# Four attention and gating layers on one core: group sums of the norm on VectorE, layer 3's values as 2x2 blocks, gamma folded into weights

## The chip, the cores and the metric

The kernel runs on one core of one Trainium2 chip. The metric is the device time of that core in microseconds (us), the median of three runs. The engines are TensorE (PE, matrix products; PEld is its weight load), VectorE (DVE), ScalarE (ACT), GpSimd (POOL) and SyncE (SP), whose queue issues nearly all of the transfers.

## The reference

The input is 16 samples of 256 channels by 32x32 positions in f32 (1024 positions a sample). Each sample passes through four layers:

- Layer 0: group norm (8 groups of 32 channels), attention over the 1024 positions with 256 channels, projection, and the sum with the input.
- Layer 1: a gate. The mean and the maximum over the channels pass through two 3x3 convolutions and a sigmoid, and the result multiplies every position.
- Layer 2: group norm and attention as in layer 0, with other weights.
- Layer 3: attention with 32-channel queries and keys, 256-channel values, a scalar gamma on the output, and the sum with the input. The kernel clips the exponentials of the scores.

```python
def _L0_conv_ref(x, gamma, beta, w_qkv, b_qkv, w_proj, b_proj):
    xn = group_norm(x, gamma, beta)                  # 8 groups of 32 channels
    q, k, v = jnp.split(einsum(xn, w_qkv) + b_qkv, 3, axis=1)
    attn = softmax(q^T k / sqrt(C))
    return einsum(attn v, w_proj) + b_proj + x
def _L1_conv_ref(x, w1, b1, w2, b2):
    weight3 = relu(conv3x3(concat[mean_c(x), max_c(x)], w1, b1))
    return x * sigmoid(conv3x3(mean_c(x) + max_c(x) + weight3, w2, b2))
def _L3_conv_ref(x, Wq, bq, Wk, bk, Wv, bv, gamma):
    ...
```

Layer 2 is as layer 0, with x + out at its end.

## The kernel before

**Streams.** The kernel is one program of generators. `sample(b)` computes a whole sample; each `yield` in it ends a step. Two streams run, `stream(0)` with the even samples and `stream(1)` with the odd ones, and `in_turn` takes a step of each in alternation; the second starts 30 steps (`OFFSET`) after the first. The steps set the order in which instructions are written; a scheduler of the framework then orders each engine's queue from it, and each engine runs its queue in order. `wait(n)` yields n empty steps, so that the other stream gets n steps ahead. The numbers of empty steps are the constants `W_PLANES`, `W_GATE1`, ..., `W_AV3` at the top. A round, in which each stream finishes one sample, repeats eight times.

**Products by seven.** `seven` (line 581) forms a product of 2x2 blocks with seven block products in place of eight, by sums of the left blocks (`s1`, `s2`, `s4`, and `s3`, which is formed in place of a block) and of the right ones (`t1`, `t2`, `t3`, `-t4`). It uses four PSUM banks (b, a, c, f); the results leave them by copies on ScalarE and by additions (`plus`) on VectorE. All of its matmuls are recorded at line 567 in `product`. In layers 0 and 2, `attend` uses it for `t` (x times the folded query-key weights), for `v` (values) and, in `logits`, for the scores of a half of the positions; `weighted` is the like for the product of the exponentials `e` with the values. Tiles whose names start with s, t or v and a bank letter (`sb_l`, `tc_l`, `va_l`) are these banks; `b_l`, `af_l`, `c_l` are those of `weighted`.

**The norm.** `group_norm` has three steps. VectorE takes statistics of each channel (`bn_stats`, `bn_aggr` into `mv`). A matmul with `gmat` (1/32 in 32x32 blocks) gives group means on every channel (`gm`, line 125); VectorE forms each channel's variance plus its squared distance from the group's mean (`d`); a second matmul sums that (`gv`, line 134). GpSimd raises to the power -1/2, and VectorE and ScalarE scale the tile. Each sample has two norms, one for layer 0 (`head`, which for sample b+2 runs in the steps of layer 3 of sample b) and one for layer 2.

**The way from tokens to channels.** The attention leaves its result with tokens in the partitions, in 32-wide strips. `turn` transposes 32x32 blocks on VectorE into a tile in slot `t` of the stream, and `send` moves the strips across partitions with one transfer for each pair of strips, sixteen in one call, from SBUF to SBUF (line 515). After layer 1 one call sends both halves; after layer 2 each half is sent when it is ready. Layer 3's tile of queries and keys (`qk`, line 1034) lies in the same slot `t`, so it may be written only when those transfers have read the slot.

**Layer 3.** `clipped_attend` (line 1028) projects a half with `w3r`, which holds the query weights twice and the key weights twice, so that each of four 32-partition groups has what it needs; ScalarE and VectorE copy queries and keys out to both partition halves (lines 1050 and 1057). The values are formed by `values_of` (line 525), eight block products without `seven`, and ScalarE multiplies them by gamma while copying (line 1061). The scores are four products of 32 rows and 512 columns at a time, in four banks (line 1074); ScalarE takes exponentials (1083) and VectorE clips them (1086).

Of the kernel before, what the change touches and what calls it, by code (L numbers as in the profile page):

```python
# [44 lines left out]
W_PLANES, W_GATE1, W_GATE2, W_SEND1 = 5, 3, 1, 8  # L45
W_NORM1, W_NORM2, W_NORM3, W_SEND2 = 6, 3, 2, 6
W_EXP, W_AV, W_AV3 = 2, 0, 0
# [11 lines left out]
class Const:  # L59


    def __init__(self, nc, pool, vecs, scal):
        self.vec = pool.tile([P, CC, NVEC], FP, name="vec")
        self.sc = pool.tile([P, NSCAL], FP, name="sc")
        self.dram = vecs, scal
        self.ident = pool.tile([P, P], FP, name="ident")
        make_identity(nc, self.ident)
        self.ones = pool.tile([P, P], FP, name="ones")
        nc.gpsimd.memset(self.ones, 1.0)

        self.gmat = pool.tile([P, P], FP, name="gmat")
        nc.gpsimd.memset(self.gmat, 0.0)
        for g in range(P // GROUP):
            s = slice(g * GROUP, (g + 1) * GROUP)
            nc.gpsimd.memset(self.gmat[s, s], 1.0 / GROUP)
        self.neg_half = pool.tile([P, CC], FP, name="neg_half")
        nc.gpsimd.memset(self.neg_half, -0.5)

        self.toep = pool.tile([P, 2 + NG, STRIP], FP, name="toep")
        self.neg_b2 = pool.tile([P, 1], FP, name="neg_b2")
# [28 lines left out]
def group_norm(nc, k, small, psum, ptag, xt, out, gamma, beta, nm, keep=None):  # L111
# [3 lines left out]
    mv = small.tile([P, CC, 2], FP, tag="mv", name=f"mv_{nm}")  # L115
    for c in range(CC):
# [4 lines left out]
        nc.vector.bn_aggr(mv[:, c, :], st[:, c, :, :])  # L121
    yield

    gm_ps = psum.tile([P, HALF], FP, tag=ptag, name=f"gm_{nm}")
    nc.tensor.matmul(gm_ps[:, :CC], k.gmat, mv[:, :, 0], start=True, stop=True)
    gm = small.tile([P, CC], FP, tag="gm", name=f"gms_{nm}")
    nc.vector.tensor_copy(gm, gm_ps[:, :CC])
    d = small.tile([P, CC], FP, tag="d", name=f"d_{nm}")
    nc.vector.tensor_tensor(d, mv[:, :, 0], gm, ALU.subtract)
    nc.vector.tensor_tensor(d, d, d, ALU.mult)  # L130
    nc.vector.tensor_tensor(d, d, mv[:, :, 1], ALU.add)
    yield
    gv_ps = psum.tile([P, HALF], FP, tag=ptag, name=f"gv_{nm}")
    nc.tensor.matmul(gv_ps[:, :CC], k.gmat, d, start=True, stop=True)
    ve = small.tile([P, CC], FP, tag="ve", name=f"ve_{nm}")
    nc.vector.tensor_scalar(ve, gv_ps[:, :CC], EPS, None, ALU.add)
    rstd = small.tile([P, CC], FP, tag="rstd", name=f"rstd_{nm}")
    nc.gpsimd.tensor_tensor(rstd, ve, k.neg_half, ALU.pow)
    a = small.tile([P, CC], FP, tag="a", name=f"a_{nm}")
# [61 lines left out]
def fast_path(nc, tc, k, bad, x, w_l0, w_l2, w_l3, qk_bias, v_bias, tap_idx, out):  # L201
# [7 lines left out]
    with ExitStack() as ctx:  # L209
# [8 lines left out]
        small = ctx.enter_context(tc.tile_pool(name="small", bufs=4))  # L218
        ps_m = ctx.enter_context(
# [56 lines left out]
        for g in range(G4):  # L276
            i = g // 2
# [112 lines left out]

        w3r = wts.tile([P, CC, P], FP, name="w3r")
        gam = k.sc[:, S_GAMMA : S_GAMMA + 1]

        def fold3():
            for g in range(G4):
                i = g // 2
                tc.keep_in_program_order(
                    nc.gpsimd.tensor_copy(
                        w3r[:, :, g * DQK : (g + 1) * DQK], w3[:, :, i * DQK : (i + 1) * DQK]
                    )  # L400
                )
            ps = bank("bias3")
            for c in range(CC):
                nc.tensor.matmul(
                    ps[:, CC : CC + 1],
                    w3r[:, c, :],
# [16 lines left out]
            nc.vector.tensor_scalar(qb[:PH], qb[:PH], DQK**-0.5, None, ALU.mult)  # L423
            nc.vector.tensor_tensor(bcol3, ps[:, :CC], vcol[:, 2, :], ALU.add)
            nc.vector.scalar_tensor_tensor(bcol3, bcol3, gam, bcol2, ALU.mult, ALU.add)
            in_strips(bcol3, bstrip3, "l3")

# [80 lines left out]
        def send(z, dst, halves):  # L508


            dst = dst.rearrange("p (h g) c n -> p g h (c n)", h=NH)
            for g in range(NG):
                for b in range(NG):
                    queue = nc.sync
                    queue.dma_start(  # L515
                        dst[b * STRIP : (b + 1) * STRIP, g, halves],
                        z[g * STRIP : (g + 1) * STRIP, halves, b],
                    )

        def values_of(src, t2, w, vt, nm):  # L520

            ps = bank(f"vps_{nm}_{t2}")
            for i in range(2):
                for c in range(CC):
                    nc.tensor.matmul(
                        ps[:, i * C : (i + 1) * C],
                        src[:, 2 * t2 + i, c],
                        w[:, c],
                        start=(c == 0),
                        stop=(c == CC - 1),  # L530
                    )
            dst = vt[:, 4 * t2 : 4 * t2 + 4, :P].rearrange("p (t j) c -> p t j c", j=CC)
            return ps.rearrange("p (t j c) -> p t j c", t=2, j=CC), dst
# [53 lines left out]
        def seven(go, copy, block, banks, left, right):  # L587
# [27 lines left out]
            go(left("s3"), right("t3"), b, fresh=False)  # L615
            plus(1, 1, b)
            copy(1, 0, b)
# [8 lines left out]
        def logits(left, tt, e, h, nm):  # L626
# [20 lines left out]
            for g in range(TPH // 2):  # L647
# [23 lines left out]
                for step, _ in enumerate(seven(go, copy, block, banks, left, right)):  # L671
                    if step >= 2:
                        m = (step - 2) * TPH + 2 * g
                        nc.scalar.activation(e[:, m : m + 2, :], e[:, m : m + 2, :], AF.Exp)  # L674
                    yield

        def weighted(e, vt, tv, y, ri, h, nm, last=None):
# [58 lines left out]
            nc.vector.tensor_tensor(s2, s1, s2, ALU.subtract)  # L736
            go(a(0, 1), vb(1, 0), af[:, 0])
            yield
            nc.vector.tensor_tensor(s4, s4, s2, ALU.subtract)
            go(a(1, 1), t4, af[:, 1])  # L740
            plus(lo, c1, af[:, 0])
# [119 lines left out]
        def checks():  # L861
# [6 lines left out]
            yield from alike(w3[:, :, 2 * DQK :], "l3")  # L868
            yield

        def attend(xt, y, weights, lane, nm, then):
# [3 lines left out]
            xs = slot("xs", lane, [P, 3, TPH, P], nm)  # L875
            s1, s2, s4 = (xs[:, i] for i in range(3))
            blocks = [[xt[:, half(h), c] for c in range(CC)] for h in range(NH)]
            s3 = blocks[1][0]
            nc.vector.tensor_tensor(s1, s3, blocks[1][1], ALU.add)
            nc.vector.tensor_tensor(s2, s1, blocks[0][0], ALU.subtract)  # L880
            nc.vector.tensor_tensor(s4, blocks[0][1], s2, ALU.subtract)
            nc.vector.tensor_tensor(s3, blocks[0][0], s3, ALU.subtract)
            left = factors(blocks, {"s1": s1, "s2": s2, "s3": s3, "s4": s4})

            def right_of(w, sums):
                return factors(
                    [[w[:, kk, j * P : (j + 1) * P] for j in range(CC)] for kk in range(CC)],
                    {
                        "t1": sums[:, 0],
                        "t2": sums[:, 1],  # L890
                        "t3": w[:, 0, P:],
                        "-t4": sums[:, 2],
                    },
                )
# [23 lines left out]

            def v_block(i, j):
                return vt[:, i * NT + j : (i + 1) * NT : CC, :P]  # L920

            def v_go(xb, wb, ps, fresh=True, lone=True):
                product(
                    [
                        (ps[:, i * P : (i + 1) * P], [(xb[:, i], wb)])
                        for i in range(TPH)
                    ],
                    fresh,
                    lone,
                )  # L930

            def v_copy(i, j, ps):
# [546 lines left out]
```

## Time and profile before

| | before |
|---|---|
| time, median of 3 (range) | 2776.7 us (2775.44 to 2781.42) |
| span of the profiled run, granted TensorE clock | 2772.2 us, 0.996 |
| HBM read, written | 36.02 MB, 16.78 MB |

The groups of instructions that the change touches (a table by line, engine, operation and shape):

| group | count | busy us | mean ns |
|---|---|---|---|
| `gm_l`, `gv_l` matmuls of two columns (125, 134) | 64, 64 | 9.2, 10.0 | 214, 226 |
| `qk` matmuls of 512 columns (1041) | 128 | 61.4 | 602 |
| `vps_l` matmuls of 256 columns (525) | 512 | 120.7 | 379 |
| `s` matmuls, 32 rows, 512 columns (1074) | 512 | 75.5 | 639 |
| ScalarE copies of queries (1050) | 64 | 43.5 | 680 |
| VectorE copies of keys (1057) | 64 | 48.4 | 756 |
| ScalarE copies of values with gamma (1061) | 64 | 43.7 | 684 |
| VectorE `bn_stats` (118) | 128 | 82.7 | 675 |
| ScalarE exponentials in layers 0 and 2 (674) | 256 | 270.2 | 1056 |
| transfers of `send`, 64 KB and 32 KB (515) | 256, 512 | | landing 2000, 1800 |

Times in such tables are busy time as the union of a group's instructions; [...]consecutive matmuls overlap, and what one costs is read from the distance between the starts of two.

### The profile page before, as it was taken

Reading aid. Unit: us, or ns where it says so; the run is one execution under the profiler, and the core shown is the slowest. Engines: PE = TensorE matmul, PEld = TensorE weight load, DVE = VectorE, ACT = ScalarE, POOL = GpSimd, SP = SyncE. Lnnn points to the kernel's source line nnn. Section 1 sums busy time; section 2 is a strip of 40 time slices with the busy share of each in tenths; the row PEclk is TensorE's granted clock in tenths of the full one; section 3 lists DMA queues with packets and bytes.
Section 4 is the critical chain, followed back from the end, with each engine's and each line's share of the span. In section 5 each row is a group of like instructions: output and inputs, shape, how many; then the busy total and the mean of one; then the engine's idle time right before and its main releaser. Section 6 shows DMA issues by size and latency. Waiting matters only on the chain.

```text
span 2772.2 us, 46004 instructions
## 1 busy us (share of the span) xinstructions
PE 2701.7 (97%) x18102; PEld 2360.8 (85%) x18102; DVE 2096.8 (76%) x4045; ACT 1319.3 (48%) x2650; POOL 56.3 (2%) x118
## 2 busy tenths in 40 slices
PE   7999999999999999999999999999999999999997
PEld 6888888888988888888788887888888888888886
DVE  7887786877778777777777868778686887777765
ACT  3444355444554445544454445454444544445443
POOL 1000000000000000000000000000000000000000
PEclk9999999999999999999999999999999999999999
DMA  4011111011110120110201102111011011100101
GB/s 112 1 31 31 39 31 32 23 31 42 28 39 22 28 60 9 39 39 16 54 12 35 39 16 54 24 23 39 23 47 31 16 39 31 39 16 16 28 20 32
DMA packets 133790, 89.43 MB, mean 32 GB/s; under 512 B 17856, under 2 KB 132800, under 8 KB 133568
## 3 DMA queue, kind: packets, MB, share of 16 engines
q1 hardware_dynamic: 131696, 85.11, 12.5%
q8 instruction: 145, 2.38, 0.4%
q10 hardware_dynamic: 1872, 1.31, 0.2%
q14 instruction: 77, 0.63, 0.1%
HBM read 36.02 MB, written 16.78 MB: 19 GB/s over the span
## 4 chain that ended last, share of the span: by engine, by line
PE 69%; DVE 15%; ACT 6%; SPq 5%; DMA 2%; issue 2%; POOL 1%; ACTq 0%; DVEq 0%
PE b_l L567 12%; PE af_l L567 10%; PE c_l L567 10%; PE sb_l L567 9%; PE sc_l L567 6%; SPq L515 5%; PE sf_l L567 3%; PE sa_l L567 3%; PE vb_l L567 3%; PE tb_l L567 2%; PE vc_l L567 2%; ACT e_l L674 2%; PE tc_l L567 2%; DVE xr L722 2%; PE s L1074 2%
## 5 line engine op out<-in xcount | busy, mean ns | idle before, releaser
L674 ACT ACTIVATE e_l<-e_l 128x1024 f32<-128x1024 f32 x256 | 270.2, 1056 | 165.6 <-DVE e_l L599 164.5
L668 ACT COPY e_l<-sb_l 128x512 f32<-128x512 f32 x384 | 220.4, 582 | 170.3 <-PE sb_l L567 106.3
L567 PE MATMUL sb_l<-t_l,x 128*128 128x256 f32 x1024 | 266.1, 388 | 0.7 <-ACT e_l L668 0.7
L567 PE MATMUL b_l<-vt,e_l 128*128 128x128 f32 x2048 | 258.7, 277 | 0.9
L567 PEld LDWEIGHTS b_l<-vt,e_l 128*128 128x128 f32 x2048 | 244.8, 192 | 12.8 <-issue 7.7
L567 PEld LDWEIGHTS sb_l<-t_l,x 128*128 128x128 f32 x1024 | 179.8, 191 | 48.7 <-ACT e_l L668 13.6
L567 PE MATMUL c_l<-tv,cb_l 128*128 128x129 f32 x1536 | 187.2, 274 | 0.0
L599 DVE TENSOR_TENSOR e_l<-sc_l,e_l 128x512 f32<-128x512 f32 x128 | 88.1, 689 | 127.4 <-PE sc_l L567 125.3
L567 PEld LDWEIGHTS c_l<-tv,cb_l 128*128 128x128 f32 x1536 | 181.5, 191 | 1.6
L746 ACT COPY acc_l<-c_l 128x256 f32<-128x256 f32 x96 | 35.8, 373 | 271.5 <-DVE ri_l L745 178.4
L1083 ACT ACTIVATE e<-s 128x512 f32<-128x512 f32 x256 | 137.0, 605 | 54.5 <-PE s L1074 54.3
L567 PEld LDWEIGHTS af_l<-vt,e_l 128*128 128x128 f32 x1024 | 123.3, 192 | 38.0 <-ACT e_l L674 26.5
L567 PE MATMUL af_l<-vt,e_l 128*128 128x128 f32 x1024 | 131.6, 278 | 21.6 <-ACT e_l L674 21.6
L471 ACT ACTIVATE xr<-xr,bstrip 128x128 f32<-128x128 f32 (+1 forms) x376 | 139.3, 436 | 3.2 <-DVE xr L478 2.6
L567 PEld LDWEIGHTS af_l<-tv,e_l 128*128 128x128 f32 x1024 | 121.2, 192 | 19.4 <-issue 19.0
L599 DVE TENSOR_TENSOR e_l<-sf_l,e_l 128x512 f32<-128x512 f32 x128 | 88.5, 691 | 61.4 <-ACT e_l L668 61.2
L567 PE MATMUL sc_l<-tc_l,xs_l 128*128 128x256 f32 x512 | 133.0, 382 | 0.0
L567 PE MATMUL sb_l<-tc_l,xs_l 128*128 128x256 f32 x512 | 132.5, 381 | 0.5 <-ACT e_l L668 0.5
L567 PE MATMUL sa_l<-t_l,x 128*128 128x256 f32 x512 | 132.1, 381 | 0.0
L567 PE MATMUL sc_l<-t_l,xs_l 128*128 128x256 f32 x512 | 131.5, 379 | 0.0
L567 PE MATMUL c_l<-vt,e_l 128*128 128x129 f32 x1024 | 127.8, 277 | 3.7 <-ACT acc_l L746 3.6
L567 PE MATMUL sf_l<-tc_l,x 128*128 128x256 f32 x512 | 131.4, 379 | 0.0
(238 smaller groups left out, 5768.7 us busy)
## 6 DMA issues: line engine op xcount, KB each, us to landing
xr<-in_x_dram SPq DMA_DIRECT2D x64, 256.0 KB, 4.9
x<-t_z SPq DMA_DIRECT2D x256, 64.0 KB, 2.0
x<-t_l SPq DMA_DIRECT2D x512, 32.0 KB, 1.8
x<-in_x_dram SPq DMA_DIRECT2D x62, 256.0 KB, 4.1
out_dram<-xr SPq DMA_DIRECT2D x124, 128.0 KB, 2.3
raw_l<-in_w_l_dram SPq DMA_DIRECT2D x1, 1024.0 KB, 6.9
raw_l<-in_w_l_dram SPq DMA_DIRECT2D x2, 256.0 KB, 5.7
raw_l<-in_w_l_dram ACTq DMA_DIRECT2D x2, 256.0 KB, 5.6
```

Source lines behind the costliest of these rows:

```text
L471: nc.scalar.activation(y[:, s, ts], y[:, s, ts], AF.Identity, bias=bias[:, s : s + 1])
L515: queue.dma_start(dst[b * STRIP : (b + 1) * STRIP, g, halves], z[g * STRIP : (g + 1) * STRIP, halves, b],)
L567: mm = nc.tensor.matmul(out, left, right, start=fresh and m == 0 and (lone or i == 0), stop=(m == len(pairs) - 1), skip_group_check=True,)
L599: nc.vector.tensor_tensor(dst, src, dst, ALU.add)
L668: nc.scalar.copy(block(i, j), ps.rearrange("p (m n) -> p m n", m=2))
L674: nc.scalar.activation(e[:, m : m + 2, :], e[:, m : m + 2, :], AF.Exp)
L722: nc.vector.scalar_tensor_tensor(to, acc[:, i, :].rearrange("p (s j) -> p s j", j=STRIP), ri[:, t : t + 1], y[:, :, t, :], ALU.mult, ALU.add,)
L746: nc.scalar.copy(acc[:, hi, c2], c[:, :, :P])
L1074: nc.tensor.matmul(ss[g], kk[gs, mm * P : (mm + 1) * P], q[gs, hs], start=True, stop=True,)
L1083: nc.scalar.activation(e[:, mm, :], ss[g], AF.Exp)
```

## The change

- **Norm.** The matmuls with `gmat` go. The channels' means and variances are put side by side in a tile of 32 columns (`moments`); VectorE's transpose turns each 32x32 block, so that the 32 channels of a group lie along a row; `bn_stats` and `bn_aggr` over the row give the mean and the variance of both columns; the result is spread over 64 columns and turned back. The group's variance is the mean of the variances plus the variance of the means. The aim is to free TensorE from a small product that waits for VectorE twice.
- **Layer 3's values** go through `seven` (`values`, shared with `attend`), with the left sums formed by `combine`. Gamma is multiplied into the value weights once, in `fold3`.
- **Layer 3's projections and scores.** `w3qk` has, for each of two pairs of position tiles, 64 output columns (queries and keys, in either order). Four products of 256 columns and 64 outputs fill the two partition halves of a bank. Queries are scaled in the weights. Scores come as eight products of 256 columns per four banks.
- **`send`** goes through a tile in DRAM: four transfers out, one of 4 KB rows back. Layer 1's two halves are sent one by one.
- **`logits` and `weighted`.** The last exponential of a half is split in two, block (1,1) first, and `weighted` uses block (1,1) before (1,0); in `seven` the last copy is written ahead of an addition.
- **Empty steps.** All of the W constants are set anew. `W_AV`, 0 before, is 2.

```diff
-W_PLANES, W_GATE1, W_GATE2, W_SEND1 = 5, 3, 1, 8
-W_NORM1, W_NORM2, W_NORM3, W_SEND2 = 6, 3, 2, 6
-W_EXP, W_AV, W_AV3 = 2, 0, 0
+W_PLANES, W_GATE1, W_GATE2, W_SEND1, W_NORM1, W_NORM2, W_NORM3, W_SEND2, W_EXP, W_AV, W_AV3 = 9, 1, 2, 4, 2, 10, 4, 7, 2, 2, 0
...
-        nc.vector.bn_aggr(mv[:, c, :], st[:, c, :, :])
+        nc.vector.bn_aggr(mv[:, 2 * c : 2 * c + 2], st[:, c, :, :])
+    nc.vector.transpose(row, mv)
     yield
-    nc.tensor.matmul(gm_ps[:, :CC], k.gmat, mv[:, :, 0], start=True, stop=True)
-    nc.vector.tensor_copy(gm, gm_ps[:, :CC])
-    nc.vector.tensor_tensor(d, mv[:, :, 0], gm, ALU.subtract)
-    nc.vector.tensor_tensor(d, d, d, ALU.mult)
-    nc.vector.tensor_tensor(d, d, mv[:, :, 1], ALU.add)
-    yield
-    nc.tensor.matmul(gv_ps[:, :CC], k.gmat, d, start=True, stop=True)
-    nc.vector.tensor_scalar(ve, gv_ps[:, :CC], EPS, None, ALU.add)
+    nc.vector.bn_stats(rst, row)
+    nc.vector.bn_aggr(rmv, rst)
+    nc.vector.tensor_copy(wide, rmv.unsqueeze(2).to_broadcast([P, 2, GROUP]))
+    nc.vector.transpose(
+        both.rearrange("p i n -> p (i n)"), wide.rearrange("p i n -> p (i n)")
+    )
+    gm = both[:, 0, 0 : 2 * CC : 2]
+    nc.vector.scalar_tensor_tensor(
+        ve, both[:, 0, 1 : 2 * CC : 2], EPS, both[:, 1, 0 : 2 * CC : 2], ALU.add, ALU.add
+    )
     nc.gpsimd.tensor_tensor(rstd, ve, k.neg_half, ALU.pow)
+    yield
...
+            wv3 = w3[:, :, 2 * DQK :]
+            nc.vector.tensor_scalar(wv3, wv3, gam, None, ALU.mult)
+            vc = right_sums(nc.gpsimd, wv3, "vc_l3")
+            folded["l3"] = wv3, vc
...
+            mid = dram.tile([n, P, NG, C], FP, tag=f"mid{n}", name=f"mid_{nm}")
             for g in range(NG):
-                for b in range(NG):
-                    queue.dma_start(
-                        dst[b * STRIP : (b + 1) * STRIP, g, halves],
-                        z[g * STRIP : (g + 1) * STRIP, halves, b],
-                    )
+                nc.sync.dma_start(
+                    mid.rearrange("h (b i) g n -> g i (h b) n", b=NG)[g],
+                    z[g * STRIP : (g + 1) * STRIP, halves].rearrange("i h b n -> i (h b) n"),
+                )
+            nc.sync.dma_start(
+                dst.rearrange("p (h g) c n -> p h (g c n)", h=NH)[:, halves],
+                mid.rearrange("h p g n -> p h (g n)"),
+            )
...
-                        nc.scalar.activation(e[:, m : m + 2, :], e[:, m : m + 2, :], AF.Exp)
+                        if step == 3 and g:
+                            for j in reversed(range(2)):
+                                part = block(1, j)
+                                nc.scalar.activation(part, part, AF.Exp)
+                        else:
+                            nc.scalar.activation(e[:, m : m + 2, :], e[:, m : m + 2, :], AF.Exp)
...
+            go(a(1, 1), t4, af[:, 1])
+            yield
             go(a(0, 1), vb(1, 0), af[:, 0])
-            yield
+            plus(lo, c1, af[:, 0])
             nc.vector.tensor_tensor(s4, s4, s2, ALU.subtract)
-            go(a(1, 1), t4, af[:, 1])
-            plus(lo, c1, af[:, 0])
...
                 for c in range(CC):
-                    nc.tensor.matmul(
-                        ps.rearrange("p (g n) -> p g n", g=TPH),
-                        w3r[:, c, :],
-                        xt[:, half(h), c],
+                    for i in reversed(range(2)):
+                        g0 = h * TPH + i * qt
+                        nc.tensor.matmul(
+                            ps[i * PH : (i + 1) * PH, : qt * P].rearrange(
+                                "p (g n) -> p g n", g=qt
+                            ),
+                            w3qk[:, c, i],
+                            xt[:, g0 : g0 + qt, c],
...
-                for t2 in range(h * TPH // 2, (h + 1) * TPH // 2):
-                    ps, dst = values_of(xt, t2, w3[:, :, 2 * DQK :], vt, f"l3_{b}")
-                    nc.scalar.activation(dst, ps, AF.Copy, scale=gam)
+                if h:
+                    combine(left)
+                yield
+                if not h:
+                    next(steps)
                     yield
+            yield from steps
...
+                    for j in range(2):
+                        for g, (_, _, blk) in enumerate(groups):
                             nc.tensor.matmul(
-                            ss[g],
-                            kk[gs, mm * P : (mm + 1) * P],
-                            q[gs, hs],
+                                ss[g][:, j * 2 * P : (j + 1) * 2 * P].rearrange(
+                                    "p (t g j) -> p t g j", t=TPH, g=2
+                                ),
+                                qk[gs, mh, 1 - blk, j * P : (j + 1) * P],
+                                qk[gs, h, blk].rearrange("p (g t j) -> p t g j", g=2, t=TPH),
```

## The prediction

> **What bounds the kernel now.** I read the page first (busy shares), then the table of groups by form, then TensorE's timeline in a steady stretch, to learn what a matmul costs when nothing is in its way, then the waits of every engine, and last the chain of waits, for the length of a round. The page, its busy shares:
>
> ```profile
> PE 2701.7 (97%) x18102; PEld 2360.8 (85%) x18102; DVE 2096.8 (76%) x4045; ACT 1319.3 (48%) x2650; POOL 56.3 (2%) x118
> ```
>
> TensorE is busy 97%, VectorE 76%, ScalarE 48%. A busy TensorE may still run below its pace, so the timeline of TensorE has to say what full pace is (start, length, instruction; the distance from one row's start to the next is the true cost):
>
> ```profile
> 1441.21 1.03 PE L567 MATMUL sb_l<-t_l,x 128*128 128x256 f32 x4
> 1442.08 1.03 PE L567 MATMUL sa_l<-t_l,x 128*128 128x256 f32 x4
> 1442.94 1.95 PE L567 MATMUL b_l<-vt,e 128*128 128x128 f32 x16
> 1444.72 1.03 PE L567 MATMUL sc_l<-tc_l,xs_l 128*128 128x256 f32 x4
> ...
> 1381.31 1.14 PE L1074 MATMUL s<-t_qk 32*128 32x512 f32 x8
> 1382.38 1.16 PE L567 MATMUL vb_l<-wvp_l,x 128*128 128x128 f32 x8
> ...
> 1366.13 0.55 PE L134 MATMUL gv_l<-d_l,gmat 128*128 128x2 f32 x2 [2.83 <-DVE d_l L131]
> ```
>
> Each f32 matmul is two records. Four records of 256 columns take 0.865 us (0.216 each), sixteen of 128 take 1.78 us (0.1115 each): 0.84 to 0.87 ns a column and pass. So the time is columns streamed, plus what TensorE waits. The eight `s` records (four products of 32 rows by 512 columns) take 1.07 us, not 3.4: four row groups run at once. The last row is a wait: the group-sum matmul `gv` held the in-order queue 2.83 us for VectorE. The waits, over the whole run (us, times, longest):
>
> ```profile
> PE af_l L567 <- ACT e_l L674: 21.6, 26, 1.1
> PE gv_l L134 <- DVE d_l L131: 14.4, 8, 2.8
> ACT t_qk L1050 <- DMA x<-t_l: 43.0, 16, 5.9
> DVE st_l L118 <- DMA x<-in_x_dram: 21.6, 18, 6.8
> ```
>
> The first two are nearly all that TensorE waits in steady state. The third is behind the second: ScalarE's copy of layer 3's queries may not overwrite slot `t` until the sixteen transfers of `send` have read it, and ScalarE stands up to 5.9 us. The chain of waits gives the length of a round (two samples, one on each stream), by the same step six rounds apart:
>
> ```profile
> 471.92 3.39 PE af_l L567 x28
> ...
> 2508.55 3.39 PE af_l L567 x28
> ```
>
> (2508.55 - 471.92)/6 = 339.4 us. In columns a sample needs: layers 0 and 2, each 14 x 0.43 + 56 x 0.1115 + 112 x 0.2165 + 224 x 0.1115 = 61.5; layer 3, 8 x 0.43 + 32 x 0.2165 + 4 x 1.2 (`s` with its entry and exit) + 25 = 40.1; gate and norm 1. That is 164 us, 328 for two: 11 us a round, 3%, are lost to waits. The change can win these 11 and whatever columns it removes; each of the eight rounds counts.
>
> **What the Trainium skill says.** "TensorE: Matmul & The Clock Gate", Part 3, says that products on different 32-row strips run at once, 3.07 times as fast for four, and puts three column tiles at 2.38 times. The trace agrees on rows (1.07 us for what would be 3.4); no run here shows columns. "TensorEngine Tiling (Array Packing)", Key Properties: changing the tiling mode drains the array; the trace has about 0.1 us at entry and 0.1 at exit of each `s` set. "VectorE: DVE Perf Modes", The three transpose paths: VectorE's transpose turns independent 32x32 blocks, which is just what a sum over groups of 32 channels needs; the trace has it at 0.69 us for 512 columns (line 503), as an addition of that size. "DMA: Bandwidth & Descriptors", Anatomy of one DMA: a fixed 2.0 us each; the trace has 1.8 to 2.3 for the small ones.
>
> **The change part by part.**
>
> *Norm.* 64 matmuls of two columns leave TensorE (groups `gm_l` 9.2 and `gv_l` 10.0 us busy; start to start in the timeline they and the gap after them take about 0.25 us each, so 16 us), and with them the wait of 14.4. After the 2.83 us wait the next two `tb_l` passes took 2.06 instead of 1.02, so the pace dropped for a moment too; I add 1. VectorE loses five small instructions of 0.16 us and gains six (two transposes of 32 and 64 columns, statistics, aggregate, copy, sum), each between 0.16 and 0.3: +0.4 us, 13 us over 32 norms, beside TensorE's work. On the norm's own path two round trips to TensorE go. **-31 us.** VectorE still waits for the loads ahead of the statistics (21.6 us in all); the other stream's additions queue behind that, as before.
>
> *Layer 3's projections.* Per half two products of 512 columns (4 x 0.43 = 1.72 us) become four of 256 columns with 64 outputs, in pairs on different column halves: 0.87 us if a pair runs at once, plus 0.2 for two changes of mode. 32 halves x -0.65 = **-21 us**. If they don't overlap: +0.2 x 32 = +6. I take the overlap, by the page and by the rows' behaviour.
>
> *Layer 3's values.* 32 records of 256 (6.93 us) become 56 of 128 (6.24): 16 x -0.69 = **-11 us**. The price is on VectorE: four `plus` and four `combine` additions of 0.69 us a sample, 88 us in all. Its copies of keys fall from 64 x 0.756 to 96 x about 0.42 (-8). VectorE goes from 2097 to about 2190 us, 81% of the new span. ScalarE: three copies of 0.59 for four of 0.68; gamma is multiplied into the weights once.
>
> *Layer 3's scores.* A set of four products of 512 columns becomes eight of 256, the same columns. A pass of the set takes 0.53 us against 0.43 for a full-array pass: 0.1 us of weight load shows. Four passes in place of two: 64 sets x 0.2 = **+13 us**. Exponentials and clips keep number and size.
>
> *Split exponential, order of `weighted`, waits.* Block (1,1) is raised as soon as it is whole and used first, while (1,0) follows; W_AV gives two steps between. The wait was 1.08 us behind eight products (1.78 us): ScalarE now has 0.6 us less ahead of that product. A quarter stays: **-16 us**. 64 extra ScalarE instructions cost about 0.2 each on an engine at 48%.
>
> *Send through DRAM.* The sixteen issues of a half took 11.04 us on the queue (0.69 each). Now four of 128 KB (0.5 each, landing 2.3 as `out_dram` does) and one of 512 KB (by the page 2.0 + 1.2; by `x<-in_x_dram` 4.1): 8 to 9.5 us to arrival instead of 12.8, and slot `t` is free after 4.3. In the new order the turn lies some 8 us of products ahead of layer 3's first projection, 4.5 before. The 43 us of ScalarE go; TensorE saw them mostly as the `gv` wait counted above. **-5 us.**
>
> *New waits.* From layer 3's first projection to its first weighted product I count in the new order 28 us of VectorE work beside 22.7 us of products (22.5 beside 25 before). Banks come free through those additions. Between 0 and 3 us at each of 16 places; I take 0.75: **+12 us.**
>
> Sum: -31 - 21 - 11 + 13 - 16 - 5 + 12 = -59; 2776.7 - 59 = **2718 us.**
>
> **The rivals.** *No column overlap* (0.20): the pair shares all 128 rows, and nothing in the trace shows such a pair. -59 + 27: 2745. *More waits vanish* (0.20): the new step counts also hide the small losses (11 us a round, of which 4.5 are counted above; 2.3 more) and VectorE's backlog never reaches TensorE: -59 - 12 - 18: 2688. For it: TensorE's waits are short and all of one kind; against: VectorE gains 4%. *VectorE binds in layer 3* (0.08): 3 us at each of 16 places (+36), statistics that hold VectorE's queue for a transfer (+15), and a pair that doesn't overlap (+27): -59 + 78, 2796, slower. For it: 28 against 22.7 us; against: the next stage has about 14 us of additions beside 24 of products, so a backlog drains.
>
> **How the numbers follow.** My forecast has 0.52, the rivals 0.20, 0.20, 0.08. Slower is the last; "same" (2771 to 2782) is its near edge and that of the second, 0.03; faster 0.89. The range takes in 2688 and 2745 with 8 to 13 us for the unknown additions: 2680 to 2758.
>
> **What would show it.** Right: no matmul of two columns in the norm; the `af` wait at a few us; `qk` half as long start to start; no ScalarE wait for `x<-t_l`; a round of about 332 us. `s` should take 1.3 us a set. Wrong: `qk` records one behind the other; TensorE waiting for VectorE at layer 3's `sc` or `b`; VectorE standing on transfers before the statistics for longer than 21.6 us.

## The result and the profile after

| | before | after |
|---|---|---|
| time, median | 2776.07 us | 2709.08 us (2705.31 to 2712.07) |
| ratio to before, 95% interval | | 0.9756 [0.9735, 0.9777] |
| span of the profiled run, granted TensorE clock | 2772.2 us, 0.996 | 2705.2 us, 0.996 |
| HBM read, written | 36.02 MB, 16.78 MB | 69.58 MB, 50.33 MB |

The kernel became 67 us faster; the forecast was 59. The page of the kernel after, its busy shares and the chain of waits by engine:

```profile
PE 2658.2 (98%) x18998; PEld 2365.2 (87%) x18998; DVE 2154.8 (80%) x4242; ACT 1323.9 (49%) x2746; POOL 45.1 (2%) x118
...
PE 82%; DVE 12%; ACT 4%; issue 1%; DMA 0%; POOL 0%; DVEq 0%; SPq 0%
```

TensorE has lost 43.5 us of busy time and VectorE has gained 58 net; four sums and four additions a sample are new to it. Of the chain that ended last, 82% is now TensorE; before it was 69%, with 5% on SyncE's queue, which issues the transfers. The chain of waits, by the same step six rounds apart:

```profile
390.66 3.57 PE b_l L571 x32
...
2372.76 3.57 PE b_l L571 x32
```

(2372.76 - 390.66)/6 = 330.35 us a round, 9.1 less than before; the forecast's sum implied 332. TensorE's timeline after, a set of `qk` and a set of `s` (start, length, instruction):

```profile
1323.05 1.08 PE L1072 MATMUL qk<-x,w3qk 128*64 128x256 f32 x8
1324.06 1.13 PE L571 MATMUL tb_l<-x,m_l 128*128 128x512 f32 x2
...
1343.09 1.15 PE L1107 MATMUL s<-t_qk 32*128 32x256 f32 x16
1344.16 1.16 PE L571 MATMUL vb_l<-wvp_l,x 128*128 128x128 f32 x8
```

A half's projection takes 1.01 us from start to start (1.72 before, as the forecast priced it), so the column halves run at once (the two records of a pair start 0.007 us apart). A set of scores takes 1.07 us, exactly as the set of four wide products did before: the forecast had 1.27. The waits after, over the run (us, times, longest):

```profile
PE b_l L571 <- ACT e_l L684: 8.9, 22, 0.7
PE b_l L571 <- DVE e L1128: 4.2, 3, 1.9
PE af_l L571 <- ACT e_l L682: 4.1, 16, 0.3
PE vc_l L571 <- DVE xs_l L902: 2.3, 1, 2.3
...
ACT t_qk L1084 <- DMA x<-mid_x: 3.9, 6, 0.7
```

`af` waits 4.1 us where it waited 21.6, `gv` is gone, and ScalarE no longer stands 43 us for `send` before it writes `t_qk`; it waits 3.9 us for the data itself. That agrees with the forecast's list of signs, but for the scores. Whether each part earned what the forecast gave it, the traces alone cannot tell: so the parts were done and undone one at a time.

### The profile page after: what moved, and what is told of

Its sections match the earlier page's. It is cut to its first block, busy times and chain, and to the rows that moved or that the text cites. A ratio compares the mean times of both kernels' runs of the same rounds, so it can differ in the third digit from the quotient of the medians.

```text
span 2705.2 us, 47663 instructions
## 1 busy us (share of the span) xinstructions
PE 2658.2 (98%) x18998; PEld 2365.2 (87%) x18998; DVE 2154.8 (80%) x4242; ACT 1323.9 (49%) x2746; POOL 45.1 (2%) x118
## 3 DMA queue, kind: packets, MB, share of 16 engines
HBM read 69.58 MB, written 50.33 MB: 44 GB/s over the span
## 4 chain that ended last, share of the span: by engine, by line
PE 82%; DVE 12%; ACT 4%; issue 1%; DMA 0%; POOL 0%; DVEq 0%; SPq 0%
PE b_l L571 16%; PE c_l L571 12%; PE af_l L571 12%; PE sb_l L571 11%; PE sc_l L571 8%; PE sf_l L571 4%; PE sa_l L571 4%; PE vb_l L571 3%; PE tb_l L571 3%; PE vc_l L571 2%; PE s L1107 2%; PE tc_l L571 2%; DVE vt L603 1%; ACT e_l L684 1%; PE qk L1072 1%
## 5 line engine op out<-in xcount | busy, mean ns | idle before, releaser
L684 ACT ACTIVATE e_l<-e_l 128x1024 f32<-128x1024 f32 x192 | 203.0, 1057 | 186.4 <-DVE e_l L603 186.4
L925 ACT COPY vt<-vb_l 128x512 f32<-128x512 f32 x144 | 84.5, 587 | 128.8 <-PE vb_l L571 127.5
L571 PE MATMUL af_l<-tv,e_l 128*128 128x128 f32 x1024 | 130.5, 276 | 4.1 <-ACT e_l L682 4.1
L571 PE MATMUL b_l<-vt,e 128*128 128x128 f32 x1024 | 127.6, 278 | 4.2 <-DVE e L1128 4.2
L571 PEld LDWEIGHTS b_l<-vt,e 128*128 128x128 f32 x1024 | 123.4, 195 | 7.3 <-DVE e L1128 5.2
L1128 DVE TENSOR_SCALAR e<-e 128x1024 f32<-128x1024 f32 x128 | 82.8, 684 | 58.9 <-ACT e L1123 58.9
```

The costliest lines, as they stand in the source:

```text
L571: mm = nc.tensor.matmul(out, left, right, start=fresh and m == 0 and (lone or i == 0), stop=(m == len(pairs) - 1), skip_group_check=True,)
L925: nc.scalar.copy(block(i, j), ps.rearrange("p (m n) -> p m n", m=TPH))
L1128: nc.vector.tensor_scalar(part, part, EXP_MIN, EXP_MAX, ALU.max, ALU.min)
```

## The experiments

Medians of four to six runs each, with the kernel before on the same chip (its medians 2775.8 to 2777.6 us). Those whose names begin with b_ add one part to the kernel before; those with a_ undo one part of the changed kernel.

### One part added to the kernel before

**b_norm: the norm alone.** `group_norm` of the changed kernel in the kernel before, all else as it was.

```diff
-    nc.tensor.matmul(gm_ps[:, :CC], k.gmat, mv[:, :, 0], start=True, stop=True)
...
-    nc.tensor.matmul(gv_ps[:, :CC], k.gmat, d, start=True, stop=True)
...
+    nc.vector.bn_stats(rst, row)
+    nc.vector.bn_aggr(rmv, rst)
+    nc.vector.tensor_copy(wide, rmv.unsqueeze(2).to_broadcast([P, 2, GROUP]))
+    nc.vector.transpose(both..., wide...)
```

> The kernel before with the norm alone turned to VectorE. Forecast's term: -31 us (16 of columns, 15 of the wait of the second group-sum matmul), so about 2745 us, and TensorE has no wait over 1 us at the start of layer 3. Rival, the wait belongs to the slow send that holds ScalarE: only the columns go, -16 us, about 2760; ScalarE's wait for x<-t_l stays near 43 us and TensorE waits at another matmul of layer 3 in place of gv.

Measured: 2809.67 us, 1.012 [1.0105, 1.0134], 33 us slower. The waits of `gm` and `gv` are gone, and others are longer. The waits of this kernel:

```profile
PE af_l L570 <- ACT e_l L677: 33.1, 32, 2.4
PE b_l L570 <- ACT acc_l L752: 14.1, 7, 2.0
PE c_l L570 <- ACT acc_l L749: 14.0, 7, 2.5
PE vb_l L570 <- ACT vt L936: 8.6, 7, 1.7
...
ACT x L148 <- DVE bb_l L146: 42.6, 16, 4.9
```

One of the seven in its timeline (in brackets, the idle time ahead and what ended it):

```profile
1361.08 0.69 POOL L140 TENSOR_TENSOR rstd_l<-ve_l,neg_half 128x2 f32<-128x2 f32 x1 [73.13 <-DVE ve_l L136]
...
1362.39 1.24 ACT L148 ACTIVATE x<-x,bb_l,a_l 128x1024 f32<-128x1024 f32 x1 [2.39 <-DVE bb_l L146]
...
1363.54 0.35 ACT L752 COPY acc_l<-b_l 128x256 f32<-128x256 f32 x1
...
1363.94 2.05 PE L570 MATMUL b_l<-vt,e_l 128*128 128x128 f32 x16 [2.00 <-ACT acc_l L752]
```

Read it from the bottom. TensorE wants a bank of the other stream's weighted sum; ScalarE's copy that frees it (L752) stands in its queue behind the norm's scaling (L148); and that one waits 2.39 us with the queue held, for the power on GpSimd and the small VectorE rows after it. In the kernel before, the same norm of the round was held up at `gv`, and the scheduler had put the scaling later in ScalarE's queue, behind four copies into `xr` and one into `vt` (three rows of its timeline, and the wait over the whole run):

```profile
1366.18 1.27 ACT L471 ACTIVATE xr<-xr,bstrip 128x128 f32<-128x128 f32 x4
1367.35 0.68 ACT L1061 ACTIVATE vt<-vps_l,sc 128x512 f32<-128x512 f32 x1
1368.27 1.24 ACT L145 ACTIVATE x<-x,bb_l,a_l 128x1024 f32<-128x1024 f32 x1 [0.25 <-DVE bb_l L143]
...
ACT x L145 <- DVE bb_l L143: 25.1, 26, 6.1
```

Over the run these waits of ScalarE on `bb` grow from 25.1 us to 42.6. A wait has moved from one of TensorE's products to ScalarE's queue, where more stands behind it. TensorE's waits listed above are some 45 us longer than in the kernel before, so that the 14 us of `gv` are more than spent. The account by the two pages: TensorE's idle time (span less busy) grows from 70.5 to 103.4 us, which is the whole 33. Its busy time stays at 2702 and 2703 us though 128 records are gone from it; the granted clock of the profiled run is 0.993 where the kernel before has 0.996, an estimated 0.003 x 2800 = 8 us of pace; what the columns gave may have gone there, which was not followed further. That a changed spacing of the steps would cure it is not shown here: the steps were not set anew for this kernel.

**b_send: the way through DRAM,** with layer 1's two halves sent one by one, as in the changed kernel.

```diff
-            for g in range(NG):
-                for b in range(NG):
-                    queue.dma_start(dst[b * STRIP : ..., g, halves], z[g * STRIP : ..., halves, b])
+            for g in range(NG):
+                nc.sync.dma_start(mid...[g], z[g * STRIP : (g + 1) * STRIP, halves]...)
+            nc.sync.dma_start(dst..., mid...)
...
                 turn(xr, z[:, h], h)
+                send(z, x1, slice(h, h + 1), f"x1_{b}_{h}")
                 yield
-            send(z, x1, slice(0, NH))
```

> The kernel before with the send through DRAM alone. Forecast's term: -5 us, about 2771, and the gv wait of 14.4 us mostly stays. Rival (the send is the cause of that wait): the gv wait falls under 3 us and ScalarE's wait for x<-t_l is gone, -20 us, about 2756.

Measured: 2754.04 us, 0.9913 [0.9898, 0.9927], 22 us faster, four times the forecast's term. ScalarE's 43 us for `x<-t_l` are gone, and with them the wait that the forecast had given to the norm: TensorE's wait at `gv` falls from 14.4 us to 0.8, though the product is still there. The row that carried 2.83 us of idle time in the kernel before (shown with the prediction) is in this kernel's timeline, and below it the wait that is left over the run:

```profile
1361.19 0.28 PE L134 MATMUL gv_l<-d_l,gmat 128*128 128x2 f32 x2
...
PE gv_l L134 <- DVE d_l L131: 0.8, 1, 0.8
```

No bracket stands behind the row now. So the wait at `gv` came from the transfers (the way and the halves one by one were not tried apart). That it came by way of ScalarE, whose copies stood behind the one that waited for them, is read from the two waits going together; the links between were not tried one by one.

**b_norm_send: both** of the diffs above.

> The kernel before with both. If the two terms add: -36 us, about 2740. If each takes away the same wait: no better than the sum less 15, about 2755 to 2760.

Measured: 2786.57 us, 1.0036 [1.0023, 1.0049]. +33 and -22 make +11, and +10.4 is what it shows: in the old order of steps the two parts together gain nothing. So the other parts, taken together, must account for 77 us, from 2786.6 to 2709.1.

### One part of the changed kernel undone

**a_oldsteps: the numbers of empty steps of before.**

```diff
-W_PLANES, W_GATE1, W_GATE2, W_SEND1, W_NORM1, W_NORM2, W_NORM3, W_SEND2, W_EXP, W_AV, W_AV3 = 9, 1, 2, 4, 2, 10, 4, 7, 2, 2, 0
+W_PLANES, W_GATE1, W_GATE2, W_SEND1 = 5, 3, 1, 8
+W_NORM1, W_NORM2, W_NORM3, W_SEND2 = 6, 3, 2, 6
+W_EXP, W_AV, W_AV3 = 2, 0, 0
```

> The changed kernel with the numbers of empty steps of before. Forecast: the step numbers serve only the wait ahead of weighted's second product, about 10 of its 16 us: 2719. Rival, the new numbers also hide VectorE's larger load and the longer way through DRAM: +30 us or more, 2739 or above, with new TensorE waits for VectorE.

Measured: 2739.68 us, 0.9862 [0.9848, 0.9877]: 31 us come back. Part of them are short waits of the kind that b_norm has:

```profile
PE af_l L573 <- ACT e_l L684: 9.5, 18, 1.0
PE c_l L573 <- ACT acc_l L758: 8.5, 7, 1.2
...
PE b_l L573 <- ACT acc_l L761: 6.1, 7, 0.9
```

These three are 20 us longer than in the changed kernel. By the profiled runs, which differ by 35 us, TensorE is idle 22 us longer and busy 13 us longer; why it is busy longer was not followed.

**a_oldexp: one exponential for the last step, and the old order of the weighted sum.** W_AV stays 2.

```diff
-                        if step == 3 and g:
-                            for j in reversed(range(2)):
-                                part = block(1, j)
-                                nc.scalar.activation(part, part, AF.Exp)
-                        else:
...
-            go(a(1, 1), t4, af[:, 1])
-            yield
             go(a(0, 1), vb(1, 0), af[:, 0])
+            yield
             nc.vector.tensor_tensor(s4, s4, s2, ALU.subtract)
+            go(a(1, 1), t4, af[:, 1])
```

> The changed kernel with one exponential of two blocks for the last step of the logits in place of two of one block, and with the order of the last two products of the weighted sum as before; the step number between exponential and weighted sum (W_AV) stays at 2. Prediction's term: the split and the new order give 16 us together with W_AV, so without them between 6 and 16 us come back, 2715 to 2725 us, as longer waits of af on e. Rival: W_AV alone carries the wait, and this takes 2708 to 2712 us.

Measured: 2746.9 us, 0.9897 [0.9883, 0.9911]: 38 us come back, the most of any part whose removal doesn't bring a long stall with it. Its waits:

```profile
PE af_l L571 <- ACT e_l L678: 22.7, 16, 1.4
PE c_l L571 <- ACT acc_l L750: 10.6, 14, 1.8
PE vc_l L571 <- DVE xs_l L896: 8.9, 9, 2.3
```

`af` stands 22.7 us again, as in the kernel before (21.6), so two empty steps alone do not carry that wait. But behind it come two that the forecast didn't price: in the changed kernel `c` waits 0.2 us for `acc` and `vc` 2.3 us for `xs`. 18.6 + 10.4 + 6.6 = 36 us, of the 44 by which the two profiled runs differ (38 by medians). That the late product causes the two others is read from their coming together. (The split and the order were undone together; which of the two does it was not tried.)

**a_oldqk: layer 3's projections and scores as before,** values still by seven.

```diff
-                for c in range(CC):
-                    for i in reversed(range(2)):
-                        nc.tensor.matmul(ps[i * PH : (i + 1) * PH, ...], w3qk[:, c, i], xt[:, g0 : g0 + qt, c], ...)
+                for c in range(CC):
+                    nc.tensor.matmul(ps..., w3r[:, c, :], xt[:, half(h), c], ...)
```

> The changed kernel with layer 3's projections and scores as before (each half by 2 products of 512 columns for all of the four copies, and the scores on the full-width q and k), values still by seven products. The two traces gave 21.7 us for the projections and 3 us for the scores in TensorE's own time over the 16 samples. Theory: TensorE sets the end in layer 3, so all of it comes back: 2731 to 2737 us. Rival: the lanes wait on ScalarE's copies and exponentials in layer 3 and the shorter projections only lengthen a wait: 2709 to 2714 us. If the scores had cost 13 us as the prediction has it, this would take 2717 us.

Measured: 2720.86 us, 0.9802 [0.9789, 0.9816]: 12 us come back, between the theory and its rival. In TensorE's own time, from start to start, the projections take 55.5 us instead of 34.8 and the scores 75.9 instead of 75.6: 21 us. By the starts of `qk` in the timeline, a round is 2.2 us longer (15 us in seven rounds); against that, the stretch from the eighth round's first projection to the end is 2.4 us shorter: the last sample's scores start 5.1 us after the start of its second half's projection, and 7.8 in the changed kernel (its `vc` waits 0.33 us for the sums here, 2.29 there). That tail is taken up in a_lastvalues. Where the rest of the 21 us went was not followed.

**a_serialqk: the same four products, one column half after the other.**

```diff
-                for c in range(CC):
-                    for i in reversed(range(2)):
+                for i in reversed(range(2)):
+                    for c in range(CC):
```

> The changed kernel with layer 3's four projections of a half issued column half by column half, not in alternation. If a pair overlaps only when neighbours in the queue lie on different column halves, most of the overlap goes: qk 1.5 to 1.7 us a half in place of 1.0, +16 to +22 us, 2725 to 2731. If TensorE takes products of the other half ahead by itself: unchanged, 2709.

Measured: 2707.07 us, 0.9755 [0.9741, 0.9768], no difference. TensorE's timeline of this kernel:

```profile
1324.29 1.09 PE L1072 MATMUL qk<-x,w3qk 128*64 128x256 f32 x8
1325.31 1.13 PE L571 MATMUL tb_l<-x,m_l 128*128 128x512 f32 x2
```

The next product starts 1.02 us later, as with alternating halves; the first records of the two halves start 0.013 us apart. The halves need not be neighbours in the queue to run at once.

**a_oldvalues: layer 3's values by eight products,** gamma at the copy, as before.

```diff
-            steps = values(lane, left, right_of(*folded["l3"]), f"l3_{b}")
+                    for i in range(2):
+                        for c in range(CC):
+                            nc.tensor.matmul(vp[:, i * C : (i + 1) * C], xt[:, 2 * t2 + i, c], w3[:, c, 2 * DQK :], ...)
```

> The changed kernel with layer 3's values as eight block products, gamma on ScalarE's copy, no added VectorE additions. Forecast: columns +11, new waits -12, so 2705 to 2712. Rival, VectorE's 88 us are hidden wholly: +11 or more, 2718 to 2724.

Measured: 2711.11 us, 0.9764 [0.9751, 0.9777]: within 2 us of the changed kernel, no more than the scatter of the runs. The round is 1.1 us longer (331.4 by the starts of `qk`), but the stretch from the eighth round's first projection to the end is 6.2 us shorter (130.6 instead of 136.8). Hence the next.

**a_lastvalues: eight products for the last sample alone.** GpSimd puts back the block of the weights that the sums had overwritten.

```diff
+            late = b == B - 1
+            if late:
+                nc.gpsimd.tensor_tensor(wv3[:, 0, P:], wv3[:, 1, P:], wv3[:, 0, P:], ALU.subtract)
+                steps = eight(xt, vt, wv3, b)
+            else:
```

> The changed kernel, but the last sample alone takes layer 3's values as eight block products, since nothing lies beside its sums on VectorE there; one GpSimd subtraction puts back the block of the weights that the sums had overwritten. Theory: by seven saves 1.1 us in each pair of samples, but the last sample's values end some 5 us later, behind VectorE's sums and with TensorE at a lower clock; this takes 2702 to 2706 us, below both the changed kernel (2709) and the one with eight products everywhere (2711). Rival: the tail is set by the exponentials and the weighted sums, and this takes 2708 to 2712 us.

Measured: 2700.27 us (2699.4 to 2701.64), 0.9727 [0.9713, 0.974], the fastest of all: 9 us under the changed kernel by medians, 5.3 by the profiled spans. (The intervals of the two ratios just overlap, the ranges of the runs don't.) TensorE's timeline in the tail of the changed kernel:

```profile
2647.01 1.08 PE L1072 MATMUL qk<-x,w3qk 128*64 128x256 f32 x8
2650.38 1.16 PE L571 MATMUL vc_l<-vc_l,xs_l 128*128 128x128 f32 x8 [2.29 <-DVE xs_l L902]
2651.37 1.83 PE L571 MATMUL vf_l<-vc_l,x 128*128 128x128 f32 x8
2653.00 1.91 PE L571 MATMUL vb_l<-vc_l,xs_l 128*128 128x128 f32 x8
2654.84 0.70 PE L1107 MATMUL s<-t_qk 32*128 32x256 f32 x4
...
2661.93 3.56 PE L571 MATMUL b_l<-vt,e 128*128 128x128 f32 x16 [1.87 <-DVE e L1128]
```

and of this one:

```profile
2646.91 1.08 PE L1097 MATMUL qk<-x,w3qk 128*64 128x256 f32 x8
2647.93 5.45 PE L1059 MATMUL vps_l<-w,x 128*128 128x256 f32 x24
2653.31 2.01 PE L1132 MATMUL s<-t_qk 32*128 32x256 f32 x32
2656.89 2.21 PE L571 MATMUL b_l<-vt,e 128*128 128x128 f32 x16 [1.57 <-DVE e L1153]
```

With no other stream left, the sums on VectorE lie open: 2.29 us of idle TensorE, after which `vf` and the next group take 1.63 and 1.84 us from start to start for what `vc` did in 0.99. The granted clock is 0.50 from 2651.5 to 2654.9 us there, and 1.00 throughout 2647 to 2661 us here. Eight products have nothing to wait for, and the first weighted product of this sample starts 10.0 us after the projection shown instead of 14.9.

**a_oldnorm: group sums on TensorE again,** new empty steps.

```diff
+    nc.tensor.matmul(gm_ps[:, :CC], k.gmat, mv[:, :, 0], start=True, stop=True)
...
+    nc.tensor.matmul(gv_ps[:, :CC], k.gmat, d, start=True, stop=True)
```

> The changed kernel with the group sums back on TensorE, all else new. Forecast's term for the norm: 16 us of columns and up to 15 of waits come back, 2725 to 2740. Rival, from the runs of the norm alone (slower by 33 us) and of the send alone (faster by 22): the wait was the send's, and the norm's matmuls are worth only their own 0.5 us a round, so 2709 to 2716; if the norm on VectorE still costs waits on ScalarE, 2700 or below.

Measured: 2933.73 us, 1.0561 [1.0547, 1.0576], 225 us slower than the changed kernel. Its waits:

```profile
PE gm_l L123 <- DVE mv_l L119: 117.8, 17, 8.3
PE tb_l L568 <- issue: 38.5, 8, 4.8
```

With two steps (W_NORM1) between the statistics and `gm`, where the kernel before has six, the product stands in TensorE's queue before its data have come, and holds it up to 8.3 us.

**a_oldnorm_fit: the same, with the old steps around the norm** (8, 6, 3, 2 for W_SEND1 and W_NORM1 to 3).

> The changed kernel with the norm's group sums as before, on TensorE, and with the step numbers around the norm as they were before (8, 6, 3, 2 for the send and the three waits of the norm); the other step numbers stay as in the changed kernel. This is the worth of the norm's edit with the waits set for it, where the run with the new step numbers held TensorE up for 6 to 8 us at each gm. Theory: the norm's edit removes from TensorE only its own columns, about half a us a norm by the runs so far, and some short waits on gm and gv, so this takes 2712 to 2725 us (3 to 15 us over the changed kernel). Rival, the prediction's own term: the norm is worth 31 us, and this takes about 2740 us. Second rival: the old waits of 11 steps against 16 cost as much here as they cost the changed kernel with all of the old step numbers, 30 us, and this takes 2740 us as well, but then its gm and gv waits are below 1 us each, while under the first rival they are 2 us and more.

Measured: 2822.61 us, 1.0163 [1.0149, 1.0177], 114 us slower than the changed kernel, outside every expectation. `gm` is no longer late in the rounds, but the product after the norm is. The stretch in windows (the window, its length, the busy time of PE, PEld, DVE, ACT and POOL, then the granted clock, the share of the DMA engines and GB/s):

```profile
1530.00:1549.00 19.00, 18.26 (x140) 17.27 (x138) 13.75 (x28) 7.45 (x16) 0.12 (x1) 1.00 0.09 28
1549.00:1562.00 13.00, 8.18 (x13) 3.29 (x12) 8.09 (x20) 5.29 (x14) 0.77 (x2) 0.74 0.00 1
```

and in the timeline:

```profile
1548.77 0.28 PE L132 MATMUL gv_l<-d_l,gmat 128*128 128x2 f32 x2
...
1552.96 0.80 DVE L142 TENSOR_SCALAR x<-x,a_l,bb_l 128x1024 f32<-128x1024 f32 x1
...
1553.57 0.42 ACT L162 COPY rows<-pl 32x16 f32<-32x16 f32 x2
...
1553.87 2.05 PE L568 MATMUL tb_l<-x,m_l 128*128 128x512 f32 x2 [4.82 <-issue]
```

After `gv` TensorE has nothing to do for 4.82 us: this stream still has to scale its tile (until 1553.76), and the other is at its gate (`rows`), which has no product ready either. The granted clock is 0.74 over that window. As this timeline reads, the step numbers of the gate (9, 1, 2) and of the norm decide together when the two streams pause, and mixing the old ones with the new makes the pauses coincide; other numbers were not tried. So neither run gives the worth of the norm's edit in the new order.

**a_oldsend: sixteen transfers for each half again,** new empty steps. Layer 1's halves stay apart, so this isn't the old send: 512 transfers of 32 KB stand after layer 1, where the kernel before has 256 of 64 KB.

```diff
-            for g in range(NG):
-                nc.sync.dma_start(mid...[g], ...)
-            nc.sync.dma_start(dst..., mid...)
+            for g in range(NG):
+                for b in range(NG):
+                    nc.sync.dma_start(dst[b * STRIP : ..., g, halves], z[g * STRIP : ..., halves, b])
```

> The changed kernel with sixteen direct transfers a half in place of the way through DRAM (layer 1's halves still sent one by one). Forecast's term: +5, 2714. Rival, the send is worth what it was alone on the kernel before: +20 or more, 2729 to 2745, with ScalarE waiting for x<-t_l again or TensorE for the arrival of the tile.

Measured: 2847.98 us, 1.0256 [1.0242, 1.027], 139 us slower than the changed kernel; the way through DRAM was worth 22 on the kernel before. Its waits, its chain by engine and its transfers after layer 1 (issues, KB each, us to landing):

```profile
PE b_l L568 <- DVE e_l L743: 49.6, 16, 5.2
...
DVE st_l L114 <- DMA x<-t_z: 105.7, 32, 6.5
...
PE 58%; DVE 16%; SPq 14%; ACT 5%; issue 4%; DMA 3%; POOL 0%; DVEq 0%; ACTq 0%
...
x<-t_z SPq DMA_DIRECT2D x512, 32.0 KB, 1.8
```

VectorE's statistics stand up to 6.5 us for the slow transfers, and the other stream's additions behind them. Two things bring that about, and they were not tried apart: the statistics come four steps after the send instead of eight, and the transfers after layer 1 are twice as many, on a queue that takes 0.63 to 0.69 us for each (10.0 and 11.04 us for sixteen); SyncE's queue is 14% of the chain here and 5% in the kernel before. So the 139 us are not the worth of the way through DRAM.

**What the three stalls cost.** The waits listed are not the whole loss of a_oldnorm, a_oldnorm_fit and a_oldsend. TensorE's idle time (span less busy, by their pages) is 142, 60 and 95 us longer than in the changed kernel, and its busy time is 85, 57 and 46 us longer, for much the same products (the first two have 128 short records more). The granted clocks are 0.964, 0.981 and 0.985 where the changed kernel has 0.996. So a long pause of TensorE costs its own length and then some pace, as in the window above.

## Why the prediction was right or wrong

The time, the direction and the round came out as forecast. The terms did so only in part, and the sum is right because its errors cancel: that is luck.

*What bounds the kernel.* Right: TensorE's columns plus a few us of waits a round. It still does, at 98%.

*Norm, -31: wrong.* The step of this term that failed is "with them the wait of 14.4 [...] On the norm's own path two round trips to TensorE go". The wait on `gv` belonged to the send: b_send removes it with the product in place. And the removal of the products, alone, costs 33 us (b_norm), because, as its timeline reads, a turn in TensorE's queue had also set when the norm's scaling enters ScalarE's queue. The forecast's 16 us of columns don't show either: TensorE's busy time there is that of the kernel before. What the forecast called "the other stream's additions queue behind that, as before" was the place to look: it is ScalarE's copies that queue, and not as before.

*Send, -5: too small.* -22 alone (the 512 KB transfer back lands in 3.3 us, where 4.1 was one of the forecast's figures). The rule to take from it: the 43 us on ScalarE's line and the 14.4 on TensorE's were one chain, and the forecast credited the chain to its last link.

*Projections, -21: right in columns* (34.8 us start to start for 256 records, 1.01 us a half where 1.07 was forecast). *Scores, +13: wrong.* The step "Four passes in place of two" took what a set needs beyond its columns, 0.2 us, as 0.1 of weight load in every pass. In the changed kernel the four passes of a set start 0.32, 0.22 and 0.22 us apart and the next product 0.32 after the last: only the first and the last pass pay 0.1, and twice as many passes cost the same 1.07 us. Together the forecast gave them -8; undone together they are worth 12 (a_oldqk), since the last sample's tail gives some of the columns back.

*Values, -11: the columns went, the time did not.* The round is 1.1 us shorter for them, and the tail 6.2 us longer, nearly what the rounds gain (a_oldvalues, a_lastvalues). The forecast had costed the sums on VectorE as lying beside TensorE's work; at the end of the last sample there is none.

*Split exponential, order and W_AV, -16: right mechanism, too small.* The `af` wait went as forecast (4.1 us left, "a quarter stays" says 5.4). Undoing split and order costs 38, with other waits behind that of `af`. W_AV alone does not carry it: `af` stands 22.7 us with it and without the split (a_oldexp), and 9.5 with the split and without it (a_oldsteps).

*Empty steps: hardly priced.* Apart from W_AV only a rival gave them something (18 us of small losses); undoing the set costs 31 us. *New waits, +12: did not come.* TensorE's waits on VectorE in layer 3 are some 9 us in all, where the kernel before has 4.

Split and order 38, steps 31, projections and scores 12 and values 2 make some 82 us, where the step from b_norm_send to the changed kernel is 77. Parts undone one by one needn't add up, and the copy that is written ahead in `seven` was not undone; but nothing large is left over. What the norm's edit is worth within the new order stays open: with its products back, each set of step numbers tried stalls for reasons of timing. To say more, the steps would have to be chosen anew for that kernel, and this wasn't tried. What is shown is that the changed kernel's set of numbers doesn't fit the old norm (a_oldnorm); for the send it isn't shown, since a_oldsend also has more transfers.

The rival in which the column pair doesn't overlap (2745) is refuted by the 1.01 us; the one in which VectorE binds (2796) by the waits. The one with more waits gone (2688) had the right idea of what the step numbers can do, and too much of it.

## What to carry to other kernels

A wait on the bound engine is the last link of a chain: before crediting its removal to the waiting product, follow it through the engines to what holds it, here the transfers that held ScalarE. In a kernel with queues in fixed order, a small product can be a pacemaker: taking it out can move what came after it ahead of another stream's work, and then the spacing has to be set again. A pause of TensorE costs more than its length, since the passes after it may run slower for a while. An exchange of columns for additions pays where another stream fills the gaps (here 1.1 us a round), and is to be dropped in the last sample, where none does.

## What the runs showed of the hardware

- Column halves run at once even if the queue doesn't alternate them: eight records of 256 columns and 64 outputs take 1.01 us in alternation and 1.02 with two products of one half ahead of the two of the other. "TensorE: Matmul & The Clock Gate" of the Trainium skill, Part 3, has matmuls in strict order of the queue; a chain of one half behind the other would take 8 x 0.216 = 1.73 us, so here the measurement decides.
- Doubling the passes within a set of 32-row products (16 records of 256 in place of 8 of 512) leaves the set at 1.07 us: the 0.2 us beyond its columns lie at its first and last pass.
- An idle stretch of 4.82 us was followed by passes at half pace: in a_oldnorm_fit passes of 512 columns then start 0.85 us apart, 0.43 before. The same page, Part 1, has the clock at half rate after an idle window of about 3.4 us, which agrees. But shorter pauses can do it too: the pause of 2.29 us in the last sample of the changed kernel was followed by a granted clock of 0.50, and the 2.83 us at `gv` in the kernel before by two passes of 512 columns in 1.85 us.
